# One buffer shared by the activations X and the second state array of the mixer, and distance matrices made inside two mixers

## The chip, the cores and the metric

The kernel runs on one core of one Trainium2 chip. The core has five engines with their own instruction queues: TensorE (PE in the profile; its weight loads are PEld), VectorE (DVE), ScalarE (ACT), GpSimd (POOL) and SyncE (SP). SyncE only issues DMA transfers here, and nearly all of the kernel's transfers go out through it, in the order in which the program lists them. The on-chip memory has 128 partitions (SBUF); matmul results land in PSUM; DRAM lies outside.

The metric is the device time of one execution in microseconds, lower is better. The kernel before takes 8552.56 us, the median of three runs (8548.31 to 8558.02). The profile is one more execution; it took 8578.09 us, with a span of 8576.3 us between its first and last instruction.

## The reference

The input x is 64 samples of 11 x 11 positions with 128 channels, float32. Four layers follow one another, each a mixer and a feed-forward part, both added to x:

```python
for l in range(4):
    x = x + conv_ref[l](_ln_c(x))          # mixer, weights of layer l
    t = x.reshape(64, 121, 128)
    t = t + ffn_ref[l](_ln_t(t))           # l=0: experts, 1 and 2: RNN, 3: spectral
    x = t.reshape(64, 11, 11, 128)
```

The mixer projects each position to 2 x 256 numbers, xc and z. In xc the 121 positions are the channels of the state-space model and the 256 features its length:

```python
xc = silu(conv1d(xc, width 3))                          # (64, 256, 121)
dts, Bs, Cs = split(x_proj(t))                          # for two directions k
delta = softplus(dts @ dt_proj + dt_b)                  # 121 x 256 per sample
h[l] = exp(delta * A) * h[l-1] + delta * Bs * xs        # 16 states per channel
y = sum_n(h * Cs) + Ds * xs;  y = y[0] + flip(y[1])
out = layernorm(y) * gelu(z) @ out_proj_w.T
```

The RNN of layers 1 and 2 multiplies the tokens by W, normalises over all tokens and samples, and runs `yt = sigmoid(wx_t + yt @ V.T)` over the 121 positions one after the other.

The spectral part of layer 3 convolves the tokens with 16 causal filters `phi` in four bands; band i sees the first 121 // (1, 2, 4, 8)[i] positions and has its own matrices `M_phi_plus[i]` and `M_phi_minus[i]` (each 16 x 128 x 128). The bands are added with four weights from a softmax of `log_weights + gumbel`, made hard.

## The kernel before

**Stages.** `metaformer_kernel` (L1340 and after) runs four times: `conv_part`, the mixer, an object `Conv` with a schedule written out by hand; then `FFN[l]`, which is `moe_layer`, `rnn_layer`, `rnn_layer` or `stu_layer`, and whose instructions a scheduler puts in order. Between them the activations lie in DRAM, in seven arrays `mid`. A mixer reads `mid[2l-1]` and writes `mid[2l]`. The feed-forward part opens a buffer `cx.X` of its own (121 partitions x 64 x 128), and its `load()` issues first the weights of the next mixer and then eight loads of 484 KB, from `mid[2l]` to X; at its end eight stores bring X to `mid[2l+1]`.

**The mixer's tiles.** The 64 samples are worked on in NC = 8 chunks of CB = 8. A chunk has two passes, one for each direction, m = 2c + k. A pass goes over the 121 channels in 61 steps of two channels, so that a chunk takes STEPS = 122 steps. The 128 partitions are 16 states x 8 samples. In step g:

- `rows(g + 3)` (L663): TensorE spreads the rows of delta, read from the buffers R, to all states in one of the PSUM tiles `da`; `exps(g + 3)` (L676): ScalarE turns them into the decay. Both run three steps ahead.
- `scan(g)` (L684): VectorE runs the recurrence along the length. Its other input is `ub`, the product of delta and xs spread to all states: `load_u` (L640) fetches a tile of four channels 14 steps ahead into one of seven buffers, by a transfer that repeats the rows, and `times_b` (L652) multiplies it by B on GpSimd 5 steps ahead.
- The states go to `self.H[dq % 2]`, where dq = 0 to 3 counts groups of 16 pairs. There are two such arrays of 128 partitions x 512 x 16; while one fills, `by_c` (TensorE, L705) sums the other over the states into `yb`, `keep_y` (L720 on VectorE, L722 on ScalarE) moves the sums to `yst`, and `store_y` (L737) writes them to DRAM in 16 small transfers, in steps 8 to 11 and 16 to 19 after the end of a second pass.

**The plan.** Everything else of a chunk is laid between these steps by `self.at(step, f)` and `self.lay`; what a step holds is issued after its scan, in the order in which it was laid. `lead(c)` reads the chunk's x (in `begin`, L199), normalises it (`stats` with L208, `scales`, `scales2`, `scales3`) and forms the convolution. `steps(c, k, ...)` makes delta for both directions, as a softplus written in parts, and cuts it into three slices of 16 bits each, `first`, `second`, `third`; with `rest` between them GpSimd subtracts what the slices before already hold. `store` writes the slices to dD and the product u to uD, from where R and `ub` are loaded again. `tail(c - 1)` ends the chunk before: for the first half of its samples the tile `ts` is loaded from sD in step 22 (L439), turned by TensorE in step 31 (L446) and added in the next (L454), and then normalised, gated and projected; the second half follows 22 steps later. All of this shares the five queues with the steps: an instruction that waits holds up whatever stands behind it on its engine.

Before the first step, `run` does `lead(0)` and the first direction of `steps(0, 0, ...)` with nothing beside them. There (`alone`) the tiles relu, abs, w and ln lie in the second array H (`self.spare[1]`), and the bias of the convolution in the first. After the last step, `last(c)` ends the last chunk with all its tiles in the first array H (`self.spare[0]`): `sides`, `load(0)`, `ahead`, `load(1)`, `finish`; `finish` writes the last two pieces to `mid`.

**The feed-forward parts.** All of them normalise X in eight groups of eight samples (`layer_norm`, L52 and L56; two table loads on ScalarE for each group). `rnn_layer` multiplies by W, runs the recurrence (L1186, L1189) and adds the result to X (L1196). `stu_layer` (L1267 to L1329) needs the product K(lag) = sum over k of weight x phi(lag, k) x M[k] for the three short bands: 105 matrices of 128 x 128, the array KD in DRAM. They are made in `stu_matrices`, which the second RNN layer calls. It first forms the weights and a 128 x 105 filter matrix W (22 transfers, some small operations), loads M in eight pieces of 2048 columns, and then hands out 64 pieces of 256 columns, one matmul and one copy on VectorE each; the recurrence takes one piece after every position:

```python
1189                nc.scalar.activation(ys[:, t, :], pst[:, j, :], AF.Sigmoid)
1190                next(beside, None)
```

Eight stores of 840 KB bring the result to KD.

Of the kernel before, what the change touches and what calls it, by code (L numbers as in the profile page):

```python
# [82 lines left out]
class Conv:  # L83
# [75 lines left out]
    def buffers(self, fixed, work, ps_f, dram):  # L159
        nc, NC = self.nc, self.NC  # L160
        self.work = work

        self.H = [fixed.tile([128, 2 * L, 16], F32, name=f"H{i}") for i in range(2)]
        self.spare = [x.rearrange("p a w -> p (a w)") for x in self.H]
        self.da = [ps_f.tile([128, 2, L], F32, name=f"da{i}") for i in range(RING)]
        self.yb = ps_f.tile([128, 8, 2, 2, 16], F32, name="yb")
        nc.vector.memset(self.yb, 0.0)
        self.Cz = [fixed.tile([128, 64, CB], F32, name=f"Cz{i}") for i in range(4)]
        self.t = fixed.tile([128, CB, L], F32, name="t")
        nc.gpsimd.memset(self.t, 1.0)  # L170
        self.xnT = [fixed.tile([C, CB, D + 2], F32, name=f"xnT{i}") for i in range(2)]
        for x in self.xnT:
# [18 lines left out]
    def lead(self, c):  # L191
# [5 lines left out]
        def begin():  # L197
            s["x"] = work.tile([D, CB, C], F32, name="x", bufs=1)
            nc.sync.dma_start(s["x"], self.src(c * CB, CB))  # L199
            if c == 0:  # L200
                s["bias"] = self.spare[0][:D, :L]
                nc.sync.dma_start(s["bias"], self.cx.a[f"L{self.l}_conv_conv_b"].to_broadcast([D, L]))
            s["st"] = work.tile([D, CB, 6], F32, name="st", bufs=1)
            s["r"] = work.tile([D, 2, CB], F32, name="r", bufs=1)

        def stats(b):
            for i in (b, b + 1):
                nc.vector.bn_stats(s["st"][:, i, :], s["x"][:, i, :])  # L208

# [4 lines left out]

        def scales2():
            self.rsqrt(s["r"], s["mv"], self.cx.eps6[:D])

# [3 lines left out]
        def normal(b):  # L221
            x, r = s["x"], s["r"]
            for i in (b, b + 1):
                nc.scalar.activation(
                    x[:, i, :], x[:, i, :], AF.Identity, bias=r[:, 1, i : i + 1], scale=r[:, 0, i : i + 1]
                )
# [47 lines left out]
    def steps(self, c, k, start, apart, late):  # L274
# [4 lines left out]
        for b in range(0, CB, 2):  # L279
# [3 lines left out]
            def tile(n, b=b):  # L283
                if alone:
                    at = 1024 * b + 512 * ("relu", "abs", "w", "ln").index(n)
                    return self.spare[1][:, at : at + 512]
                tag, bufs = ("abs", 1) if n == "ln" else (n, 2 if n == "relu" else 1)
# [310 lines left out]


    def pairs(self):  # L600
        for m in range(2 * self.NC):
# [155 lines left out]
    def run(self):  # L757
# [14 lines left out]
        for c in range(NC):  # L772
            s = STEPS * c
            if c + 1 < NC:
# [64 lines left out]
        ahead()  # L839
        load(1)  # L840
        finish()


# [16 lines left out]
def moe_layer(cx, l, load):  # L860
# [6 lines left out]
    with ExitStack() as ctx:  # L867
# [22 lines left out]
        pooled = keep.tile([C, E, NB], F32, name="pooled")  # L890
        made = load()
        act_tables(nc, 6)

# [150 lines left out]

def stu_matrices(cx, l, keep, work, ps):


    nc, a, ident = cx.nc, cx.a, cx.ident
    p = f"L{l}_ffn_"
    phi, T3, CC, PC = a[p + "phi"], BANDS[3][0], 2048, 256  # L1050
    sw = scale_weights(cx, l, keep)
# [21 lines left out]
    nc.vector.tensor_add(ws[:, 0:1], ws[:, 1:2], mine[:, 3:4])  # L1073
    W = keep.tile([128, R0[3]], F32, name="W")
    for z in range(3):
        nc.vector.tensor_scalar_mul(W[:, R0[z] : R0[z] + NZ[z]], F[:, : NZ[z]], ws[:, z : z + 1])

    def pieces():
        loaded = {}

        def load(c0):
            loaded[c0] = m = work.tile([128, CC], F32, name="m", bufs=3)
            for i in range(4):
                for f0, src in ((0, a[p + "M_phi_plus"]), (16, a[p + "M_phi_minus"])):
                    nc.sync.dma_start(
                        m[32 * i + f0 : 32 * i + f0 + 16], src[i].rearrange("k d e -> k (d e)")[:, c0 : c0 + CC]
                    )

        load(0)
        load(CC)  # L1090
        yield
        for c0 in range(0, C * C, CC):
            if c0 + 2 * CC < C * C:
                load(c0 + 2 * CC)
            ka = work.tile([R0[3], CC], F32, name="ka", bufs=2)
            for j in range(0, CC, PC):
                pa = ps.tile([R0[3], PC], F32, name="pa", tag="mm")
                nc.tensor.matmul(pa, W, loaded[c0][:, j : j + PC], start=True, stop=True)
                nc.vector.tensor_copy(ka[:, j : j + PC], pa)
                yield  # L1100
            nc.sync.dma_start(cx.KD[:, c0 : c0 + CC], ka)

    return pieces()


def rnn_layer(cx, l, load):
# [4 lines left out]
    with ExitStack() as ctx:  # L1111
# [62 lines left out]
        for t0 in range(0, D, TS):  # L1174
# [8 lines left out]
            for j in range(n):  # L1183
# [5 lines left out]
                nc.scalar.activation(ys[:, t, :], pst[:, j, :], AF.Sigmoid)  # L1189
                next(beside, None)  # L1190
        for b in range(0, NB, 4):
# [158 lines left out]
def metaformer_kernel(ctx: ExitStack, tc: tile.TileContext, a: dict, out: bass.AP):  # L1350
# [23 lines left out]

    cx.KD = dram.tile([sum(t1 for _, t1 in BANDS[:3]), C * C], F32, name="KD")
    v, kept, passing, weights = mixer(0)
    weights()()
    passing.close()
    for l in range(4):
        conv_part(cx, v)  # L1380
        kept.close()
        if l < 3:
            v, kept, passing, weights = mixer(l + 1)
        with tc.tile_pool(name=f"X{l}", bufs=1) as pool:
            cx.X = pool.tile([D, NB, C], F32, name="X")
            dst = outr if l == 3 else mid[2 * l + 1]
# [9 lines left out]
            for b0 in range(0, NB, GB):  # L1396
                nc.sync.dma_start(dst[:, b0 : b0 + GB, :], cx.X[:, b0 : b0 + GB, :])
        if l < 3:
# [60 lines left out]
```

## Time and profile before

| | |
|---|---|
| median of 3 runs | 8552.56 us (8548.31 to 8558.02) |
| profiled execution, its own time | 8578.09 us |
| its span | 8576.3 us |
| mean granted TensorE clock | 0.771 |
| busy: TensorE / VectorE / ScalarE / GpSimd | 6028.0 / 6122.9 / 5803.0 / 5868.7 us |
| moved by DMA | 1605.20 MB, mean 187 GB/s |

The stretches of the profiled execution, with busy times of each engine inside them (us):

| stretch | length | PE | DVE | ACT | POOL | DMA share |
|---|---|---|---|---|---|---|
| mixer 0, from 130 on | 1638 | 1136 | 1379 | 1287 | 1395 | 0.89 |
| experts, 1768 to 2050 | 282 | 217 | 104 | 77 | 18 | 0.57 |
| mixer 1, 2050 to 3816 | 1766 | 1188 | 1433 | 1358 | 1462 | 0.85 |
| RNN 1, 3816 to 4028 | 212 | 158 | 60 | 67 | 0 | 0.14 |
| mixer 2, 4028 to 5795 | 1767 | 1198 | 1433 | 1359 | 1463 | 0.87 |
| RNN 2, 5795 to 6088 | 293 | 196 | 92 | 92 | 0 | 0.32 |
| mixer 3, 6088 to 7853 | 1765 | 1200 | 1433 | 1359 | 1463 | 0.85 |
| spectral, 7853 to 8576 | 723 | 677 | 132 | 131 | 0 | 0.10 |

How to read it: a busy share near one in a stretch makes that engine the stretch's limit; where all shares are low, the stretch is set by waits, and the instructions ahead of which an engine stood still have to be found. In the view of the span in 40 slices each digit is the busy share of one slice of 214 us in tenths:

```profile
PE   5667777666666777666567667766577777766999
DVE  5888888843888888872788888883388888886211
ACT  6878888732788788762778888863387888885210
POOL 6888888911888888850888888870388888883000
DMA  6899999945889889960889999972488888896001
```

Lines of the profile that name an operation give line, engine, operation, output tile and input tile. A line of the timeline begins with start and duration in us and ends, in brackets, with the time that the engine stood still before it and what ended that.

### The profile page before, as it was taken

The page shows a single profiled execution, that of the slowest core. Times are in us where ns is not written, and L with a number is a line of the kernel's source. Part 1 is how long each engine was busy: PE and PEld are TensorE (multiplying, and loading weights), DVE is VectorE, ACT ScalarE, POOL GpSimd, SP SyncE. Part 2 cuts the span into 40 slices and gives each one's busy share as a digit, 9 for nine tenths or more (in the row PEclk, how much of TensorE's full clock was granted, in tenths as well). Part 3 has the DMA queues.
Part 4 walks back from the last instruction along what each step waited for, and adds up shares of the span by engine and source line. Part 5 has one row for each costly group of instructions (what it writes and reads, how often), then busy time and mean ns, then how long its engine had stood idle before and what let it go on. Part 6 is the DMA issues. An engine that isn't in the chain of part 4 may idle for free.

```text
span 8576.3 us, 209337 instructions
## 1 busy us (share of the span) xinstructions
PE 6028.0 (70%) x83432; PEld 3462.5 (40%) x83432; DVE 6122.9 (71%) x8654; ACT 5803.0 (68%) x12946; POOL 5868.7 (68%) x3171
## 2 busy tenths in 40 slices
PE   5667777666666777666567667766577777766999
PEld 3333334345333444344233334443334444433445
DVE  5888888843888888872788888883388888886211
ACT  6878888732788788762778888863387888885210
POOL 6888888911888888850888888870388888883000
PEclk7777777777787777776677777766677777777999
DMA  6899999945889889960889999972488888896001
GB/s 171 221 222 226 224 223 222 231 121 167 214 224 224 220 222 223 228 175 23 208 219 225 223 223 223 227 197 62 138 219 219 229 225 224 221 230 151 0 4 36
DMA packets 927599, 1605.20 MB, mean 187 GB/s; under 512 B 140075, under 2 KB 612755, under 8 KB 924755
## 3 DMA queue, kind: packets, MB, share of 16 engines
q1 hardware_dynamic: 925339, 1589.70, 74.3%
q8 instruction: 655, 10.73, 0.6%
q14 instruction: 325, 2.66, 0.1%
q10 hardware_dynamic: 1280, 2.10, 0.1%
HBM read 1301.02 MB, written 290.52 MB: 186 GB/s over the span
## 4 chain that ended last, share of the span: by engine, by line
PE 31%; ACT 20%; DMA 18%; DVE 14%; issue 8%; POOL 7%; SPq 2%; DVEq 0%; POOLq 0%; ACTq 0%
DVE H L684 8%; ACT da L676 7%; DMA ub<-uD 5%; POOL ub L652 5%; PE yb L705 4%; PE da L663 4%; DMA ts<-sD 4%; PE pc L244 3%; DMA uD<-u 3%; PE acc L1290 3%; PE out L1329 2%; PE pu L1287 2%; PE pst L1186 2%; PE po L500 2%; DMA R<-dD 2%
## 5 line engine op out<-in xcount | busy, mean ns | idle before, releaser
L652 POOL TENSOR_TENSOR ub<-ub,Bt 128x1024 f32<-128x1024 f32 (+1 forms) x1984 | 4565.9, 2318 | 749.7 <-DMA ub<-uD 545.4
L684 DVE TENSOR_TENSOR_SCAN H<-da,ub 128x512 f32<-128x512 f32 (+1 forms) x3904 | 4495.2, 1197 | 248.8 <-POOL ub L652 120.6
L676 ACT ACTIVATE da<-da,A 128x255 f32<-128x255 f32 x7744 | 3392.4, 447 | 1122.2 <-PE da L663 936.6
L663 PE MATMUL da<-R,pick 120*128 120x255 bf16 x7744 | 1787.7, 325 | 956.2 <-DVE H L684 761.0
L705 PE MATMUL yb<-H,Cz 128*16 128x64 f32 x65536 | 1722.6, 250 | 557.4 <-ACT yst L722 367.7
L705 PEld LDWEIGHTS yb<-H,Cz 128*16 128x16 f32 x65536 | 1165.4, 111 | 1603.6 <-issue 837.7
L663 PEld LDWEIGHTS <-pick 120*128 120x128 bf16 x7744 | 602.4, 105 | 1657.0 <-issue 781.4
L720 DVE TENSOR_TENSOR yst<-yst,yb 128x512 f32<-128x512 f32 (+2 forms) x640 | 340.5, 549 | 277.4 <-PE yb L705 277.3
L170 POOL MEMSET t<- 128x2048 f32 x4 | 7.2, 1805 | 716.2 <-DMA x<-mid 703.1
L244 PE MATMUL pc<-w_conv,xnT 128*121 128x256 f32 x1344 | 445.5, 429 | 56.4 <-ACT t L248 56.4
L722 ACT COPY yst<-yb 128x512 f32<-128x512 f32 (+2 forms) x640 | 330.8, 543 | 112.0 <-DMA yD<-yst 50.0
L295 PE MATMUL pd<-t,w_dt 122*128 122x512 f32 x480 | 355.4, 832 | 57.4 <-ACT t L255 57.4
L327 POOL TENSOR_TENSOR u<-relu,t 128x512 f32<-128x512 f32 x240 | 307.4, 1281 | 22.2 <-DVE relu L318 22.2
L336 POOL TENSOR_TENSOR d<-relu,d 128x512 bf16<-128x512 f32 x240 | 279.0, 1163 | 59.2 <-ACT d L333 59.2
L1267 DVE COPY U<-pu 128x488 f32<-128x488 f32 x128 | 85.3, 666 | 296.6 <-PE pu L1287 277.2
L1269 ACT COPY U<-pu 128x488 f32<-128x488 f32 x128 | 72.9, 570 | 311.8 <-PE pu L1287 304.9
L330 POOL TENSOR_TENSOR relu<-relu,d 128x512 f32<-128x512 f32 x240 | 279.3, 1164 | 6.6
L244 PEld LDWEIGHTS pc<-w_conv,xnT 128*121 128x121 f32 x1344 | 234.7, 209 | 103.4 <-ACT t L248 82.2
L629 POOL TENSOR_TENSOR Cz<-Cp,own 128x512 f32<-128x512 f32 x256 | 274.3, 1071 | 0.0
L361 PE MATMUL pb<-t,x_bc 121*64 121x512 f32 x256 | 174.6, 771 | 132.0 <-ACT bc L366 100.9
L314 DVE SCALAR_TENSOR_TENSOR pd<-w,pd 128x512 f32<-128x512 f32 x240 | 163.8, 683 | 103.2 <-ACT w L307 103.0
L401 PE MATMUL pg<-xnT,in_zT 128*128 128x484 f32 x256 | 156.2, 695 | 110.1 <-ACT g L412 101.2
(238 smaller groups left out, 7509.7 us busy)
## 6 DMA issues: line engine op xcount, KB each, us to landing
ub<-uD SPq DMA_DIRECT2D x1920, 512.0 KB
dD<-d SPq DMA_DIRECT2D x256, 384.0 KB
R<-dD SPq DMA_DIRECT2D x192, 420.0 KB
uD<-u SPq DMA_DIRECT2D x256, 256.0 KB
sD<-s SPq DMA_DIRECT2D x128, 256.0 KB
yD<-yst SPq DMA_DIRECT2D x512, 60.5 KB
ts<-sD SPq DMA_DIRECT2D x56, 512.0 KB
y<-yD SPq DMA_DIRECT2D x112, 242.0 KB
```

The costliest lines, as they stand in the source:

```text
L244: nc.tensor.matmul(pc, lhs, rhs, start=(j == 0), stop=(j == taps - 1))
L295: nc.tensor.matmul(s["p"], self.w_dt[:, k, :], tb[: D + 1], start=True, stop=True)
L327: nc.gpsimd.tensor_mul(s["u"], s["relu"], tb)
L330: nc.gpsimd.tensor_sub(s["relu"], s["relu"], s["d"][:, 0, :])
L336: nc.gpsimd.tensor_sub(s["d"][:, 2, :], s["relu"], s["d"][:, 1, :])
L652: self.nc.gpsimd.tensor_mul(x, x, self.bc[m, "Bt"].unsqueeze(1).to_broadcast([128, n, L]))
L663: self.nc.tensor.matmul(self.da[g % RING][:, j, 1:], self.pick[:n, d % 5].rearrange("p n b -> p (n b)"), self.R[m, d // 35][:n, d % 35 // ...
L676: self.nc.scalar.activation(x, x, AF.Exp, scale=self.A[:, m % 2, d : d + 1])
L684: self.nc.vector.tensor_tensor_scan(self.H[dq % 2][:, :n, p - DQ[dq][0]], self.da[g % RING].rearrange("p j l -> p (j l)")[:, :n], x.rearra ...
L705: self.nc.tensor.matmul(self.yb[32 * q : 32 * q + 16, slot % 8, :, :, :w], self.Cz[slot // 8][:, place % 64 : place % 64 + 2, :].rearrange ...
L720: nc.vector.tensor_add(dst, dst, src)
L722: nc.scalar.copy(dst, src)
```

## The change

The diff does four things.

**X shares the place of the second H.** A buffer HX of 128 x 8192 numbers is allocated once. The mixer uses it as `H[1]`, the feed-forward part as `cx.X`. X's loads move out of the feed-forward's `load()` into the end of `run`: seven of them behind `load(1)`, the eighth behind `finish()`. `load()` now issues only the next mixer's weights.

**The first chunk comes from X.** In mixers 1 to 3 `begin` of chunk 0 issues no load; statistics and normalisation read `cx.X`. The bias moves to `yst`, the four `alone` tiles to the first array H, since HX now still holds X. An explicit load of ScalarE's table set 6 is added in `scales2` of chunk 0.

**Distance matrices in two mixers.** `stu_matrices` loses its pieces and becomes `stu_filters`, called by `moe_layer` ahead of its normalisations; its W goes to a buffer that lives through the kernel. In mixers 1 and 2 each chunk makes two of the 32 pieces of 512 columns, with 16 loads of 32 KB in step 19, both pieces' matmuls, copies and stores from step 25 on (23 steps later in chunk 0), with tiles that carry the tags relu, w and abs of `steps`. `rnn_layer` has nothing beside its recurrence any more.

**First slices on VectorE.** In the `alone` part, w, `rest` and `third` go from ScalarE and GpSimd to VectorE.

```diff
@@ buffers
-        self.H = [fixed.tile([128, 2 * L, 16], F32, name=f"H{i}") for i in range(2)]
+        self.H = [fixed.tile([128, 2 * L, 16], F32, name="H"), cx.HX.rearrange("p (a w) -> p a w", w=16)]
@@ lead
         def begin():
-            s["x"] = work.tile([D, CB, C], F32, name="x", bufs=1)
-            nc.sync.dma_start(s["x"], self.src(c * CB, CB))
+            s["x"] = s["in"] = work.tile([D, CB, C], F32, name="x", bufs=1)
+            if c == 0 and self.l > 0:
+                s["in"] = self.cx.X[:, :CB, :]
+            else:
+                nc.sync.dma_start(s["x"], self.src(c * CB, CB))
             if c == 0:
-                s["bias"] = self.spare[0][:D, :L]
+                s["bias"] = self.yst.rearrange("p a d -> p (a d)")[:D, :L]
...
-                nc.vector.bn_stats(s["st"][:, i, :], s["x"][:, i, :])
+                nc.vector.bn_stats(s["st"][:, i, :], s["in"][:, i, :])
...
         def scales2():
+            if c == 0:
+                act_tables(nc, 6)
             self.rsqrt(s["r"], s["mv"], self.cx.eps6[:D])
@@ steps
-                    return self.spare[1][:, at : at + 512]
+                    return self.spare[0][:, at : at + 512]
...
-                nc.scalar.activation(s["w"], s["p"], AF.Identity, bias=self.one)
+                if alone:
+                    nc.vector.tensor_scalar_add(s["w"], s["p"], 1.0)
+                else:
+                    nc.scalar.activation(s["w"], s["p"], AF.Identity, bias=self.one)
...
             def rest(s=s):
-                nc.gpsimd.tensor_sub(s["relu"], s["relu"], s["d"][:, 0, :])
+                less = nc.vector if alone else nc.gpsimd
+                less.tensor_sub(s["relu"], s["relu"], s["d"][:, 0, :])
...
             def third(s=s):
-                nc.gpsimd.tensor_sub(s["d"][:, 2, :], s["relu"], s["d"][:, 1, :])
+                less = nc.vector if alone else nc.gpsimd
+                less.tensor_sub(s["d"][:, 2, :], s["relu"], s["d"][:, 1, :])
@@ new function of Conv
+    def matrices(self, i):
+        nc, a, s = self.nc, self.cx.a, {}
+        cols = slice(512 * i, 512 * i + 512)
+        def load():
+            tag = ("relu", "w")[i % 2]
+            s["m"] = self.work.tile([128, 512], F32, name="m", tag=tag, bufs=2 - i % 2)
+            for j in range(4):
+                for f0, M in ((0, a["L3_ffn_M_phi_plus"]), (16, a["L3_ffn_M_phi_minus"])):
+                    nc.sync.dma_start(
+                        s["m"][32 * j + f0 : 32 * j + f0 + 16], M[j].rearrange("k d e -> k (d e)")[:, cols]
+                    )
+        def add():
+            s["p"] = self.ps.tile([R0[3], 512], F32, name="pk", tag="mm")
+            nc.tensor.matmul(s["p"], self.cx.W, s["m"], start=True, stop=True)
+        def leave():
+            s["k"] = self.work.tile([R0[3], 512], F32, name="ka", tag="abs", bufs=1)
+            nc.scalar.copy(s["k"], s["p"])
+        def store():
+            nc.sync.dma_start(self.cx.KD[:, cols], s["k"])
+        return load, add, leave, store
@@ run
+            if self.l in (1, 2):
+                for i in range(2):
+                    for step, f in zip((19, 25, 26, 27), self.matrices(2 * (NC * (self.l - 1) + c) + i)):
+                        self.at(s + step + (3 * i if step > 19 else 0) + (23 if c == 0 else 0), f)
             if c > 0:
...
         load(1)
+        X = self.cx.X
+        for c in range(NC - 1):
+            self.nc.sync.dma_start(X[:, CB * c : CB * c + CB, :], self.dst(CB * c, CB))
         finish()
+        self.nc.sync.dma_start(X[:, CB * NC - CB :, :], self.dst(CB * NC - CB, CB))
@@ moe_layer
         made = load()
+        stu_filters(cx, 3, keep)
         act_tables(nc, 6)
@@ stu_matrices becomes stu_filters(cx, l, keep)
-    W = keep.tile([128, R0[3]], F32, name="W")
+    W = cx.W
...
-    def pieces():
-        loaded = {}
-        def load(c0):
-            loaded[c0] = m = work.tile([128, CC], F32, name="m", bufs=3)
-            for i in range(4):
-                for f0, src in ((0, a[p + "M_phi_plus"]), (16, a[p + "M_phi_minus"])):
-                    nc.sync.dma_start(
-                        m[32 * i + f0 : 32 * i + f0 + 16], src[i].rearrange("k d e -> k (d e)")[:, c0 : c0 + CC]
-                    )
-        load(0)
-        load(CC)
-        yield
-        for c0 in range(0, C * C, CC):
-            if c0 + 2 * CC < C * C:
-                load(c0 + 2 * CC)
-            ka = work.tile([R0[3], CC], F32, name="ka", bufs=2)
-            for j in range(0, CC, PC):
-                pa = ps.tile([R0[3], PC], F32, name="pa", tag="mm")
-                nc.tensor.matmul(pa, W, loaded[c0][:, j : j + PC], start=True, stop=True)
-                nc.vector.tensor_copy(ka[:, j : j + PC], pa)
-                yield
-            nc.sync.dma_start(cx.KD[:, c0 : c0 + CC], ka)
-    return pieces()
@@ rnn_layer
-        beside = stu_matrices(cx, l + 1, keep, work, ps) if l == 2 else iter(())
...
-                next(beside, None)
@@ metaformer_kernel
+    hold = ctx.enter_context(tc.tile_pool(name="hold", bufs=1))
+    cx.HX = hold.tile([128, NB * C], F32, name="HX")
+    cx.X = cx.HX[:D].rearrange("p (b c) -> p b c", c=C)
+    cx.W = const.tile([128, R0[3]], F32, name="W")
...
-            cx.X = pool.tile([D, NB, C], F32, name="X")
...
-            def load():
-                made = weights() if l < 3 else None
-                for b0 in range(0, NB, GB):
-                    nc.sync.dma_start(cx.X[:, b0 : b0 + GB, :], mid[2 * l][:, b0 : b0 + GB, :])
-                return made
-            FFN[l](cx, l, load)
+        FFN[l](cx, l, weights if l < 3 else lambda: None)
```

More of the change, by code (lines that the diff above doesn't have):

```diff
@@ L159, in buffers @@
     def buffers(self, fixed, work, ps_f, dram):
-        nc, NC = self.nc, self.NC
+        cx, nc, NC = self.cx, self.nc, self.NC
         self.work = work
-        self.H = [fixed.tile([128, 2 * L, 16], F32, name=f"H{i}") for i in range(2)]
+        self.H = [fixed.tile([128, 2 * L, 16], F32, name="H"), cx.HX.rearrange("p (a w) -> p a w", w=16)]
         self.spare = [x.rearrange("p a w -> p (a w)") for x in self.H]
@@ L224, in normal @@
                 nc.scalar.activation(
-                    x[:, i, :], x[:, i, :], AF.Identity, bias=r[:, 1, i : i + 1], scale=r[:, 0, i : i + 1]
+                    x[:, i, :], s["in"][:, i, :], AF.Identity, bias=r[:, 1, i : i + 1], scale=r[:, 0, i : i + 1]
                 )
@@ L1042, with stu_filters @@
 R0 = (0, NZ[0], NZ[0] + NZ[1], NZ[0] + NZ[1] + NZ[2])
-def stu_matrices(cx, l, keep, work, ps):
+def stu_filters(cx, l, keep):
     nc, a, ident = cx.nc, cx.a, cx.ident
     p = f"L{l}_ffn_"
-    phi, T3, CC, PC = a[p + "phi"], BANDS[3][0], 2048, 256
+    phi, T3 = a[p + "phi"], BANDS[3][0]
     sw = scale_weights(cx, l, keep)
@@ L1373, in mixer @@
         return v, kept, passing, lambda: v.weights(setup, pool, ps)
-    cx.KD = dram.tile([sum(t1 for _, t1 in BANDS[:3]), C * C], F32, name="KD")
+    hold = ctx.enter_context(tc.tile_pool(name="hold", bufs=1))
+    cx.HX = hold.tile([128, NB * C], F32, name="HX")
+    cx.X = cx.HX[:D].rearrange("p (b c) -> p b c", c=C)
+    cx.W = const.tile([128, R0[3]], F32, name="W")
+    cx.KD = dram.tile([R0[3], C * C], F32, name="KD")
     v, kept, passing, weights = mixer(0)
@@ L1383, in metaformer_kernel @@
             v, kept, passing, weights = mixer(l + 1)
-        with tc.tile_pool(name=f"X{l}", bufs=1) as pool:
-            cx.X = pool.tile([D, NB, C], F32, name="X")
-            dst = outr if l == 3 else mid[2 * l + 1]
-            def load():
-                made = weights() if l < 3 else None
-                for b0 in range(0, NB, GB):
-                    nc.sync.dma_start(cx.X[:, b0 : b0 + GB, :], mid[2 * l][:, b0 : b0 + GB, :])
-                return made
-            FFN[l](cx, l, load)
-            for b0 in range(0, NB, GB):
-                nc.sync.dma_start(dst[:, b0 : b0 + GB, :], cx.X[:, b0 : b0 + GB, :])
+        dst = outr if l == 3 else mid[2 * l + 1]
+        FFN[l](cx, l, weights if l < 3 else lambda: None)
+        for b0 in range(0, NB, GB):
+            nc.sync.dma_start(dst[:, b0 : b0 + GB, :], cx.X[:, b0 : b0 + GB, :])
         if l < 3:
```

## Prediction

> **What bounds the kernel now.** I read the page's slices first, then the boundaries between layers in order of time, then one pass of the mixer loop. The slices show two kinds of time. In the mixers VectorE, ScalarE, GpSimd and the DMA engines are all eight or nine tenths busy; around slices 9, 18, 27 and from 36 on, where the feed-forward layers stand, nearly all but TensorE fall away. There a transfer or a serial chain sets the end.
>
> The two RNN layers run the same code, except that the second also makes the distance matrices. Here is each one's first normalisation, last sigmoid and last addition, as lines of single source lines (first and last start in us):
>
> ```profile
> L52 DVE BATCH_NORM_STATS2 ln_st<-X x64: 259/277/296, 3830.4 to 3862.4; 121x6 f32<-121x128 f32 x64
> L1189 ACT ACTIVATE ys<-pst x121: 224/224/224, 3878.3 to 4012.9; 128x64 f32<-128x64 f32 x121
> L1196 DVE TENSOR_TENSOR X<-X,px x16: 686/687/689, 4014.5 to 4026.9; 121x512 f32<-121x512 f32 x16
> ...
> L52 DVE BATCH_NORM_STATS2 ln_st<-X x64: 258/275/294, 5835.5 to 5884.7; 121x6 f32<-121x128 f32 x64
> L1189 ACT ACTIVATE ys<-pst x121: 224/224/225, 5904.4 to 6043.4; 128x64 f32<-128x64 f32 x121
> L1196 DVE TENSOR_TENSOR X<-X,px x16: 686/687/689, 6074.8 to 6087.2; 121x512 f32<-121x512 f32 x16
> ```
>
> At the boundaries the timeline (start, duration, engine, line) shows what was waited for, in the brackets:
>
> ```profile
> 3816.09 0.24 DVE L157 TENSOR_REDUCE own<-ident 128x8 f32<-128x128 f32 x1
> 3830.42 1.65 DVE L52 BATCH_NORM_STATS2 ln_st<-X 121x6 f32<-121x128 f32 x8 [1.32 <-DMA X<-mid]
> ...
> 5835.52 1.65 DVE L52 BATCH_NORM_STATS2 ln_st<-X 121x6 f32<-121x128 f32 x8 [8.24 <-DMA X<-mid]
> 5838.48 1.28 ACT L56 ACT_TABLE_LOAD   x1
> ...
> 2057.55 1.64 DVE L208 BATCH_NORM_STATS2 st<-x 121x6 f32<-121x128 f32 x8 [7.96 <-DMA x<-mid]
> 4038.06 1.64 DVE L208 BATCH_NORM_STATS2 st<-x 121x6 f32<-121x128 f32 x8 [9.78 <-DMA x<-mid]
> 6097.77 1.65 DVE L208 BATCH_NORM_STATS2 st<-x 121x6 f32<-121x128 f32 x8 [9.13 <-DMA x<-mid]
> ```
>
> Both ways across a boundary the activations are stored and loaded again, and VectorE idles for it. Last, the place in the mixer loop where the new matrix steps land, in its second pass in layer 1:
>
> ```profile
> 2378.72 3.02 SPq L737 DMA_DIRECT2D yD<-yst  x4
> 2382.46 1.56 SPq L613 DMA_DIRECT2D R<-dD  x1
> 2386.46 0.90 SPq L439 DMA_DIRECT2D ts<-sD  x1
> 2396.83 1.07 PE L446 MATMUL pk<-ident,ts 121*128 121x121 f32 x4 [5.52 <-DMA ts<-sD]
> 2397.94 0.66 DVE L454 TENSOR_TENSOR y<-y,pk 128x484 f32<-128x484 f32 x1 [6.70 <-PE pk L446]
> ```
>
> SyncE is issuing almost without a gap and runs behind; ts lands 10.4 us after its issue, and TensorE, then VectorE, stand for it. This place is already late.
>
> **The change, part by part** (times on the profiled execution, 8578.1 us around a span of 8576.3).
>
> *X loaded at the mixer's end.* Seven of X's eight loads (484 KB each) now go out behind the last yD loads, while the mixer finishes; the eighth waits for the last store. VectorE's preparation of the next layer ends at 3816.33 in RNN 1, and the statistics start at 3830.42: 14.1 us go. In the expert layer: 1768.25 to 1783.49, 15.2. In the last layer X was behind 3 MB of M and MU; its first filter matmul is at 7892.1 and needs X and the filters. The filters' last VectorE step ends near 7877.5 and their own DMA does not move forward, so I take 15 (8 to 20). What the loads move past: the last two stores to mid, nothing on the path, and the weights' DMAs, which now wait about 3 us for the eighth load. Their first consumers stand behind two normalised groups.
>
> *Matrices out of RNN 2.* Its start to statistics goes from 5796.34 to 5835.52, 39.2 us, the filters' 22 DMAs and X. Its statistics to last table load before the recurrence (3870.6, 5895.9) take 40.2 us in RNN 1 and 60.3 in RNN 2: 20.1 more, since every normalisation loads two tables, 16 of 1.28. The recurrence up to the last sigmoid is 5.3 longer (142.3, 147.5); from there to the first addition 31.4 against 1.6, leftover pieces: 29.8. The sum is 94.4 us; all of it is alone on the path, so RNN 2 becomes RNN 1.
>
> *The filters in the expert layer.* There ScalarE gets 7 more table loads (by the changed program's instruction order) at 1.28: 9.0 us, and VectorE some 25 operations of 0.16, 4 us. ScalarE is some 55% busy in that phase, so between none and all 13 lands on the path; I take 5. The 22 DMAs stand ahead of the first expert weights on SyncE and cost 16.5 us of issue there (5795.6 to 5812.1 in RNN 2). Cover: the weights issued first have landed by 1830, and the expert matmuls start near 1888; without that cover it would be some 8 us.
>
> The Trainium skill ("ScalarE: Activation LUTs", What ACT_TABLE_LOAD costs) adds a drain of 1.38 us to each switch; the rows here show none, the activation behind the load at 5838.48 starts at 5839.77. With it the seven would be 18.6 instead of 9.0 and that layer would gain nothing.
>
> *First chunk from X.* Three mixers start without the reload: 8.0, 9.8 and 9.1 by the brackets (less 0.0 to 0.2 of other waiting): 26.9 us. The bias load no longer waits and is needed 16 us later. The added table load in scales2 I cost at nothing: in the changed order the same two loads still stand before r's Ln and Exp in these mixers.
>
> *First slices on VectorE.* In the prologue of layer 1 the first dD store is issued at 2099.29, the last at 2114.56. In between GpSimd serialises u (1.28), rest and third (1.15 each) and two waits for dD landings of 2.95. With the subtractions at 0.69 (VectorE's rows of this shape) off GpSimd, the two rounds shorten by about 1.1 and 3.2: 4 us a mixer, 16 in all (bounds 4 and 24). Moving w to VectorE saves ScalarE 0.69 a tile, but ln then waits for another engine: nothing. VectorE gets 12 operations, 8.3 us, in a stretch where it is half idle.
>
> Gains: 14.1 + 15.2 + 15 + 94.4 − 5 + 26.9 + 16 = 176 us (150 to 192).
>
> *The matrices in mixers 1 and 2.* Sixteen times: 16 loads of 32 KB and two stores of 215 KB on SyncE, two matmuls (near 0.8), two copies on ScalarE (0.57). The 16 loads go ahead of R, dD, uD, ub and ts. At RNN 2's spacing of 0.46 us that is 7.4 us of issue, where SyncE has no gap. On the data side 0.94 MB at the rate of RNN 2's burst (193 GB/s at 76% share) is 3.7 us. So ts lands between 2.2 us (its 512 KB share of bytes alone) and 7.4 us (issue alone) later. The second copy reuses the one buffer of the first and waits, three pairs after it, for that store to land: stores here take 6 to 8 us (uD, bcD), 3.5 of which pass meanwhile and three pairs of decay are ready ahead (3.6), so 0 to 4 more; behind it on ScalarE stand the exponentials, and VectorE for them. Lower bound: all of it inside idle time, 0. Upper: 7.4 + 4 + 2.7 of added engine work, 14 us. I take 6 in the fourteen passes with a tail, nearer the DMA row than the issue row since the queue is full there, and 3 in the two first passes, where SyncE waits 18 us on VectorE at that place: 14 × 6 + 2 × 3 = 90 us.
>
> A rule speaks against these loads: the skill's page "DMA: Bandwidth & Descriptors" (Bandwidth) says that transfers below 64 KB are dominated by descriptors, and its table gives about 0.8 us for 32 KB, an estimate between two of its lines. One after the other that is 13 us a pass, 208 in all, and the change would lose some 30 us. No row of this trace has such a load, so it is not settled.
>
> Sum: 176 − 90 = 86 us off. The profiled execution lies 25.5 us above the median of 8552.56; the same sum is taken off both: 8492 profiled, **8467 us** median.
>
> **Rivals.** *The matrix steps hide*: each costs 1.5 us, 24 in all, time 8401. For it: SyncE stands 873 us of 1630 in layer 1's mixer waiting for VectorE, so delays are made up. Against: GpSimd is full outside the stalls. *SyncE's hold starves the loop*: ub and R arrive late as well, GpSimd stops, and each pass pays 13 us: 176 − 208, time 8585, slower. It decides from 11 us a pass (176 / 16). For it: POOL already waits 3.2 us for ub at 2394.55; against: five tiles stand between its load and its use. *The expert layer takes back its gain*: ScalarE's sqrt waits for filter DMAs and the normalisations behind it stand 15 us instead: 25 us worse, 8492. That the change does not do what it says is excluded for RNN 2, whose order has no pieces left.
>
> **How the numbers follow.** Forecast 0.50, hidden 0.22, starved 0.18, expert layer 0.10. The forecast's own range, 3 to 9 us a pass, is 8421 to 8515. The range 8405 to 8560 takes in half of the hidden case and all but the worst of the starved one. A difference of 0.2% (17 us) is about what can be told from none. Faster: 0.50 + 0.22 + 0.10 less 0.06 for bad ends, 0.76; same 0.06; slower 0.18.
>
> **What would show it.** Statistics within 3 us of `own` at RNN layers; RNN 2 from own to last addition as long as RNN 1, near 197 us; no x wait before L208's successor; last dD store 11 us behind the first. In mixers 1 and 2 a pass of 215 us instead of 209, with the wait for ts near 8 us. Wrong if those mixers grow by over 170 us together or by under 40.

## The result and the profile after

The changed kernel takes 8643.77 us, the median of four runs (8635.67 to 8652.78), against 8552.01 before (now four runs): 1.0107 times as long, with an interval of 1.0089 to 1.0124. The forecast was 8467 and faster; it is slower by 92 us. The profiled execution took 8652.78 us around a span of 8651.0.

Stretch by stretch, from the starts of the first normalisation and the first scan and the ends of the last scan and the last addition in the two traces (us; a feed-forward part runs from the mixer's end to the next mixer's first statistics):

| stretch | before | after | difference |
|---|---|---|---|
| experts, RNN 1, RNN 2 | 290.7, 223.1, 303.1 | 296.2, 206.9, 213.2 | +5.5, −16.2, −89.9 |
| spectral part | 723.4 | 704.2 | −19.2 |
| prologues of the four mixers | 67.5, 69.4, 69.5, 71.4 | 66.1, 67.5, 67.2, 68.2 | −8.8 together |
| loops of mixers 0 and 3 | 1647.6, 1645.2 | 1642.2, 1636.2 | −14.4 |
| loops of mixers 1 and 2 | 1649.1, 1648.7 | 1755.2, 1759.2 | +216.6 |

Mixers 0 and 3 do the same work in both kernels; their 14.4 us fit a profiled execution of before that was on the long side of its runs, as its 25.5 us above the median said.

What was to be gained was mostly gained. The groups of single lines in the RNN layers, after (min/median/max ns, first and last start):

```profile
L52 DVE BATCH_NORM_STATS2 ln_st<-HX x64: 255/276/298, 3923.7 to 3949.9; 121x6 f32<-121x128 f32 x64
L1207 ACT ACTIVATE ys<-pst x121: 224/224/225, 3974.8 to 4110.5; 128x64 f32<-128x64 f32 x121
...
L52 DVE BATCH_NORM_STATS2 ln_st<-HX x64: 254/276/296, 6000.3 to 6026.6; 121x6 f32<-121x128 f32 x64
L1207 ACT ACTIVATE ys<-pst x121: 224/224/224, 6053.0 to 6188.8; 128x64 f32<-128x64 f32 x121
L1213 DVE TENSOR_TENSOR HX<-HX,px x16: 686/687/689, 6190.3 to 6202.7; 121x512 f32<-121x512 f32 x16
```

RNN 2 now runs like RNN 1, and its additions follow the last sigmoid at once. The way from the first statistics to the first sigmoid grew, though: 51.1 us in RNN 1 against 47.9 before, and 52.7 in RNN 2. The timeline at the boundaries:

```profile
3920.06 0.24 DVE L157 TENSOR_REDUCE own<-ident 128x8 f32<-128x128 f32 x1
3923.65 1.64 DVE L52 BATCH_NORM_STATS2 ln_st<-HX 121x6 f32<-121x128 f32 x8 [3.35 <-DMA mid<-xo]
...
5991.96 0.24 DVE L157 TENSOR_REDUCE own<-ident 128x8 f32<-128x128 f32 x1
6000.26 1.65 DVE L52 BATCH_NORM_STATS2 ln_st<-HX 121x6 f32<-121x128 f32 x8 [8.06 <-DMA mid<-xo]
...
4125.77 1.58 DVE L211 BATCH_NORM_STATS2 st<-HX 121x6 f32<-121x128 f32 x8
```

The wait for x is gone from the mixers' first statistics (no bracket). The wait for X at the feed-forward's start is not gone: the mixer's last store has taken its place, with 3.4 to 8.1 us. From `own` to the start of the last addition RNN 2 takes 210.7 us, where the prediction's sign was near 197.

The loss lies in mixers 1 and 2, at one place of each chunk. At that place before, GpSimd and SyncE stood as follows:

```profile
2387.96 12.35 SPq L640 DMA_DIRECT2D ub<-uD  x5
2394.55 2.34 POOL L652 TENSOR_TENSOR ub<-ub,Bt 128x1024 f32<-128x1024 f32 x1 [3.22 <-DMA ub<-uD]
```

The five issues in 12.35 us take some 0.5 us each; in between SyncE stands 8.0 us before the last of them. So its queue has hardly a gap up to about 2389, the stretch whose lines the prediction shows, and it has a large one right behind. SyncE's timeline in mixer 1 after, at the same place:

```profile
2383.80 0.89 SPq L775 DMA_DIRECT2D yD<-yst  x2
2384.74 0.74 SPq L620 DMA_DIRECT2D m<-in_L_ffn_M_phi_plus_dram  x1
...
2393.59 0.42 SPq L620 DMA_DIRECT2D m<-n_L_ffn_M_phi_minus_dram  x1
2394.06 0.70 SPq L775 DMA_DIRECT2D yD<-yst  x2
2394.86 0.69 SPq L678 DMA_DIRECT2D ub<-uD  x1
...
2399.18 0.72 SPq L449 DMA_DIRECT2D ts<-sD  x1
...
2403.05 0.35 SPq L633 DMA_DIRECT2D KD<-ka  x1
```

Sixteen loads of m stand for 9.3 us between two stores; the next ub load waits behind them, and the first KD store goes out 6.4 us after its copy on ScalarE had ended (2396.68). GpSimd, ScalarE, TensorE and VectorE in the same timeline:

```profile
2383.56 9.34 POOL L690 TENSOR_TENSOR ub<-ub,Bt 128x1024 f32<-128x1024 f32 x4
2401.89 2.35 POOL L690 TENSOR_TENSOR ub<-ub,Bt 128x1024 f32<-128x1024 f32 x1 [8.99 <-DMA ub<-uD]
...
2396.09 0.59 ACT L630 COPY ka<-pk 105x512 f32<-105x512 f32 x1
...
2415.51 0.59 ACT L630 COPY ka<-pk 105x512 f32<-105x512 f32 x1 [12.14 <-DMA KD<-ka]
...
2417.49 1.21 PE L249 MATMUL pc<-w_conv,xnT 128*121 128x256 f32 x2 [13.01 <-ACT t L253]
...
2419.55 0.66 DVE L464 TENSOR_TENSOR y<-y,pk 128x484 f32<-128x484 f32 x1 [13.93 <-PE pk L456]
```

GpSimd stands 8.99 us for ub (3.22 before). Then ScalarE stands 12.14 us before its second copy, until the store of the first has left the only ka buffer. Behind that copy on ScalarE wait the exponentials and the copy of t (L253); for t TensorE stands 13.01 us, behind it stands the turning of ts (pk), and VectorE, which waits for pk, makes no scan from 2405.6 to 2420.1.

### The profile page after: what moved, and what is told of

Read it like the earlier page. It is cut to its first block, busy times and chain, and to the rows that moved or that the text cites. A ratio compares the mean times of both kernels' runs of the same rounds, so it can differ in the third digit from the quotient of the medians.

```text
span 8651.0 us, 209519 instructions
## 1 busy us (share of the span) xinstructions
PE 6035.8 (70%) x83368; PEld 3463.3 (40%) x83368; DVE 6128.1 (71%) x8638; ACT 5798.6 (67%) x12955; POOL 5834.6 (67%) x3139
## 4 chain that ended last, share of the span: by engine, by line
PE 30%; ACT 19%; DMA 18%; DVE 14%; issue 9%; POOL 7%; SPq 3%; DVEq 0%; POOLq 0%; ACTq 0%
ACT da L714 7%; DVE H L722 5%; DMA ub<-uD 5%; POOL ub L690 4%; PE da L701 4%; PE yb L743 4%; DVE HX L722 4%; PE pc L249 3%; PE acc L1307 2%; PE pu L1304 2%; PE out L1346 2%; DMA KD<-ka 2%; PE pst L1204 2%; DMA ts<-sD 2%; DMA yD<-yst 2%
## 5 line engine op out<-in xcount | busy, mean ns | idle before, releaser
L722 DVE TENSOR_TENSOR_SCAN H<-da,ub 128x512 f32<-128x512 f32 x2048 | 2391.7, 1205 | 110.6 <-POOL ub L690 60.9
L722 DVE TENSOR_TENSOR_SCAN HX<-da,ub 128x512 f32<-128x512 f32 (+1 forms) x1856 | 2117.7, 1187 | 206.9 <-ACT da L714 167.0
L743 PE MATMUL yb<-H,Cz 128*16 128x64 f32 x32768 | 872.2, 255 | 325.9 <-ACT yst L760 248.6
L743 PE MATMUL yb<-HX,Cz 128*16 128x64 f32 x32768 | 852.1, 246 | 195.6 <-ACT yst L760 90.3
L743 PEld LDWEIGHTS yb<-H,Cz 128*16 128x16 f32 x32768 | 607.6, 112 | 927.1 <-issue 536.7
L743 PEld LDWEIGHTS yb<-HX,Cz 128*16 128x16 f32 x32768 | 560.3, 110 | 668.3 <-issue 310.3
L346 POOL TENSOR_TENSOR d<-relu,d 128x512 bf16<-128x512 f32 x240 | 279.1, 1163 | 56.1 <-ACT d L342 55.9
```

What stands on the lines that cost most here:

```text
L346: less.tensor_sub(s["d"][:, 2, :], s["relu"], s["d"][:, 1, :])
L722: self.nc.vector.tensor_tensor_scan(self.H[dq % 2][:, :n, p - DQ[dq][0]], self.da[g % RING].rearrange("p j l -> p (j l)")[:, :n], x.rearra ...
L743: self.nc.tensor.matmul(self.yb[32 * q : 32 * q + 16, slot % 8, :, :, :w], self.Cz[slot // 8][:, place % 64 : place % 64 + 2, :].rearrange ...
```

## The experiments

Two explanations of the 216.6 us. S: the single ka buffer, ScalarE waiting for a store. Q: the queue, 16 loads holding up SyncE. Each ratio is to runs of the kernel before on the same chip, which took 8553 to 8566 us from chip to chip; between chips the ratios compare better than the medians.

**Two places for ka** (`e1`):

```diff
-            s["k"] = self.work.tile([R0[3], 512], F32, name="ka", tag="abs", bufs=1)
+            tag = ("abs", "relu")[i % 2]
+            s["k"] = self.work.tile([R0[3], 512], F32, name="ka", tag=tag, bufs=1 + i % 2)
```

> The second result tile ka of a chunk gets a place of its own (the free one of the two relu tiles), nothing else. In the changed kernel ScalarE stands 166.0 us in 16 waits, 10.4 us a chunk, before its second copy until the first KD store has landed. Theory S (that wait is the price): chunks of mixers 1 and 2 fall from 223 us to 213 to 215, and the time from 8643.8 to about 8500 (8480 to 8530). Theory Q (the 16 loads on SyncE hold up ub, R and ts, as the rival of the prediction had it): the wait goes, but GpSimd's wait for ub stays the limit, chunks stay above 219 and the time above 8585.

8536.18 us, ratio 0.9970 (0.9958 to 0.9983). ScalarE's wait is gone (no bracket at the second copy), but GpSimd still stands for ub at that place:

```profile
2365.67 9.33 POOL L691 TENSOR_TENSOR ub<-ub,Bt 128x1024 f32<-128x1024 f32 x4
2384.19 2.36 POOL L691 TENSOR_TENSOR ub<-ub,Bt 128x1024 f32<-128x1024 f32 x1 [9.18 <-DMA ub<-uD]
2385.83 0.59 ACT L631 COPY ka<-pk 105x512 f32<-105x512 f32 x1
```

**Four loads for sixteen** (`e2`), with the filter matrix's rows put in the same order:

```diff
-            for j in range(4):
-                for f0, M in ((0, a["L3_ffn_M_phi_plus"]), (16, a["L3_ffn_M_phi_minus"])):
-                    nc.sync.dma_start(s["m"][32 * j + f0 : 32 * j + f0 + 16], M[j].rearrange("k d e -> k (d e)")[:, cols])
+            for f0, M in ((0, a["L3_ffn_M_phi_plus"]), (64, a["L3_ffn_M_phi_minus"])):
+                nc.sync.dma_start(s["m"][f0 : f0 + 64], M.rearrange("j k d e -> (j k) (d e)")[:, cols])
```

> The 16 loads of a chunk (32 KB each) become 4 of 128 KB with the same bytes, by another order of the filter matrix's rows; ka keeps its single place. At the 0.46 us spacing of these issues 12 fewer are 5.5 us less SyncE time a chunk. Theory Q: chunks fall by more than 8 us, time below 8515. Theory S: the second copy still waits for the first store, which only goes out some 3 to 5 us sooner, chunks fall by 2 to 5 us, time 8560 to 8610.

8556.58 us, ratio 0.9994 (0.9985 to 1.0004): 87 us gone. ScalarE's wait fell from 166.0 to 106.7 us in all, since the store goes out sooner: in the change it started 3.6 us after its copy (median of 16 chunks), here at once in 14 of the 16. It still held the buffer 12.7 us from its issue to the second copy, against 13.5 in the change.

**Both** (`e3`):

> Both edits at once. If the two costs add, chunks come to within 2 us of the 209.5 of the kernel before and the time to about 8450 (8430 to 8480). If one of them hides behind the other (both theories partly wrong), the time is no better than the better of the two single edits.

8446.77 us, ratio 0.9866 (0.9851 to 0.9881), 1.3% faster than before. The two costs add: 107.6 + 87.2 = 194.8 singly, 197.0 together (by the ratios 117 + 97 against 206). So S and Q were both half right.

**The matrices back in RNN 2** (`e4`; all else as in the change):

> Only the matrices go back to where they were (filters and pieces in RNN 2, 64 pieces beside the recurrence); X shared, first chunk from X and the prologue's VectorE edits stay. By the changed kernel's trace the loops of mixers 1 and 2 are 106.1 and 110.5 us longer than before, RNN 2 with its neighbours 89.9 shorter, the expert layer 5.5 longer. So this kernel should have chunks of 209.5 again and take about 8450 (8430 to 8480), faster than both others. If the time stays above 8530, the loops are slowed by the shared place of H and X and not by the matrices.

8453.22 us, ratio 0.9879 (0.9862 to 0.9895), as expected, with loops of 1639.1 and 1646.3 us. So the shared place costs nothing that shows, and everything but the matrices is worth 106 us. Moving the matrices as e3 does adds hardly more (e3 against e4: 6 us, inside the intervals). By the two traces this is a balance: RNN 2 takes 206 us in e3 against 269 in e4, but the loops of mixers 1 and 2 are 31 us longer and the expert layer 28.

**Each load cut in two** (`e12`, on top of e1):

```diff
+                    for h in (0, 8):
+                        nc.sync.dma_start(s["m"][32 * j + f0 + h : 32 * j + f0 + h + 8], M[j].rearrange("k d e -> k (d e)")[h : h + 8, cols])
```

> The kernel with two ka places and the 16 loads of 32 KB, each load cut in two of 8 rows: 32 loads of 16 KB, the same bytes and the same 2 KB rows. From 16 to 4 loads 89 us went, 0.47 us for each load less in each of 16 chunks. If the number of issues on SyncE is the price, 16 more cost another 16 x 16 x 0.46 = 118 us: about 8655 (8630 to 8680). If it was the size of each transfer or the number of rows in it that mattered only between 32 and 128 KB, or the queue has room, the time stays below 8580.

8608.49 us, ratio 1.0054 (1.0039 to 1.0068): 0.0084 above e1, 72 us. More issues cost more, though less than 118, and the traces show most of why: the loads follow each other at 0.338 us (median) with 8 rows, 0.463 with 16 and 0.694 with 64, so that 32 loads of 8 rows take 3.4 us a chunk more than 16 of 16, some 54 us in all. In the table, the starts of the scans are averaged over chunks 1 to 6 of mixers 1 and 2 (a whole chunk from its first to its last scan's start), and SyncE's time for m, the sum of the loads' own durations, over 16 chunks (us):

| kernel | SyncE's time for m | steps 28 to 34 | whole chunk |
|---|---|---|---|
| before | 0 | 15.8 | 208.9 |
| e3, 4 loads, two ka | 2.7 | 18.6 | 210.1 |
| e1, 16 loads, two ka | 8.0 | 23.8 | 216.3 |
| e12, 32 loads, two ka | 10.5 | 28.3 | 220.8 |
| e2, 4 loads, one ka | 2.7 | 26.0 | 217.9 |
| after, 16 loads, one ka | 7.4 | 31.6 | 224.1 |

The steps outside 28 to 34 take the same time in all six within 2 us, so one place pays for everything. With two ka it pays 2.8, 8.0 and 12.5 us for 4, 16 and 32 loads, about what SyncE needs for them or somewhat more.

**The filters in the expert layer.** e4 has no filters there: 268.7 us; e3 296.3. The seven traces with the filters at this place and X loaded by the mixer (the change, e1, e2, e3, e7, e12, e14) lie between 289.5 and 296.4, 293.4 on average, so e3 is on the long side, and the price is 25 us rather than 28. The intervals of the ratios of e3 and of the next runs overlap; what tells them apart is the length of the layer, from one trace each. On top of e3:

```diff
 e5   stu_filters(cx, 3, keep) called behind the gating loop
 e9   -    nc.scalar.activation(sq, sq, AF.Sqrt)   (twice)
      +    nc.scalar.activation(sq, sq, AF.Ln)
      +    nc.scalar.activation(sq, sq, AF.Exp, scale=0.25)
 e11  e5 + e9, and one load each for F, sq and the sign row sg[64:128]
 e13  e11, and nc.gpsimd.memset(sg[64:128, 1:T3:2], -1.0) in place of the sign row's load
```

> On top of the kernel with two ka places and merged loads, the filters of the spectral part are made behind the gating loop of the expert layer instead of ahead of its normalisations. In the changed kernel that layer took 296.2 us from the mixer's end to the next statistics against 290.7 before, although its own statistics start 8.0 us sooner and the reload behind it (8.0) is gone: some 21 us went to the filters, 13.3 of them in one stand of VectorE for the sign row's transfer, 3.8 of ScalarE for sigma's. If the place of the filters is the cause, the layer comes to about 275 and the time to 8426 (8415 to 8436). If the 22 transfers cost the layer wherever they are issued, or the experts wait for their weights instead, it stays within 8 us of 8447.

8438.22 us, ratio 0.9853 (0.9838 to 0.9868), layer 286.2: at best half of what was hoped for. The scheduler issued the same loads right behind the mixer's weights again, so the late place was late in the program only.

> On top of two ka places and merged loads, sigma to the power 1/4 is formed by Ln and Exp instead of two square roots; the filters stay ahead of the normalisations. The expert layer with filters took 296.3 us against 268.7 in the kernel whose filters stay in RNN 2, 27.6 more, and seven table loads of 1.283 (9.0 us) are among it, since after the square root the normalisations alternate between two tables. If the tables are a third of the price, the layer comes to 286 to 288 and the time to 8438 (8430 to 8443). If only the waits for the transfers count, nothing changes (8447 within 6).

8438.45 us, ratio 0.9855 (0.9840 to 0.9869), layer 285.6: about a third of the price, as expected for the tables.

> The same, with the filters made behind the gating loop as well. That place alone was worth 8.6 us. If the two add, the layer comes to 276 to 278 and the time to 8429 (8420 to 8435); if the late place had gained by the tables alone, it equals the run with Ln and Exp.

8428.79 us, ratio 0.9840 (0.9822 to 0.9857), layer 278.9: the two add, as far as one trace tells.

> The same again, and the filters' 20 loads of phi, sigma and sign rows become 3. The experts' first weights then go out some 17 issues of 0.46 us, 8 us, sooner. If that is what is left, the layer comes to 268 to 271 and the time to 8421 (8412 to 8428), the fastest so far. If it is not, the time is that of the run before within 5.

8438.72 us, ratio 0.9856 (0.9842 to 0.9871): a miss, the layer went up to 293.0. The timeline of this run:

```profile
1776.59 0.66 SPq L1106 DMA_DIRECT2D sg<-in_sgn_dram  x1
1804.53 0.22 DVE L1109 TENSOR_TENSOR F<-F,sg 128x60 f32<-128x60 f32 x1 [22.84 <-DMA sg<-in_sgn_dram]
```

One transfer of 64 x 60 single numbers kept VectorE, and the gating behind it, until 27.9 us after its issue.

> The run with 3 filter loads, with the sign row no longer loaded but written by GpSimd (odd columns to -1). In the run with 3 loads that transfer was issued at 1776.6 and VectorE stood 22.8 us for it until 1804.5, and the expert layer took 293.0 us, 14 more than with 20 loads. If the sign row is what is left of the filters' price, the layer comes to 268 to 272 us, that of the kernel whose filters stay in RNN 2 (268.7), and the time to 8415 (8405 to 8425). If something else holds the layer, it stays above 280 and the time above 8425.

8419.71 us, ratio 0.9845 (0.9830 to 0.9861), layer 266.2: without the sign row's transfer nothing is left of the filters' price. This is the lowest median of all; its ratio does not tell it from those of the other four, but its interval ends at 0.9861, just below e4's, which begins at 0.9862. Whether the rewritten filters would shorten RNN 2 in e4 as well was not tried.

**The other parts, undone one at a time on top of e3.** e6 loads the first chunk from DRAM again, e7 puts w back to ScalarE and rest and third to GpSimd, e8 puts X's loads back behind the next mixer's weights, e14 puts all eight behind the mixer's last store:

```diff
 e14
-        for c in range(NC - 1):
-            self.nc.sync.dma_start(X[:, CB * c : CB * c + CB, :], self.dst(CB * c, CB))
         finish()
-        self.nc.sync.dma_start(X[:, CB * NC - CB :, :], self.dst(CB * NC - CB, CB))
+        for c in range(NC):
+            self.nc.sync.dma_start(X[:, CB * c : CB * c + CB, :], self.dst(CB * c, CB))
```

> On top of two ka places and merged loads, mixers 1 to 3 load their first chunk from DRAM again, as before. The prediction priced that at 8.0 + 9.8 + 9.1 = 26.9 us; if that holds the time is 8474 (8466 to 8481). If the load hid behind the bias load or the table load anyway, it is within 8 us of 8447.

8474.72 us, ratio 0.9891 (0.9874 to 0.9907), 28 above e3 by the medians, 21 by the ratios: near the 26.9 that were predicted.

> On top of two ka places and merged loads, the prologue's w goes back to ScalarE and rest and third to GpSimd. The prediction priced the move at 4 us in each of four mixers, 16 together; the traces before and after show the stretch from first statistics to first scan shorter by 1.4, 2.0, 2.2 and 3.2 us, 8.8 together. By the prediction 8463, by the traces 8456. Within 4 us of 8447 would say that the waits for dD and ub set the prologue either way.

8454.92 us, ratio 0.9875 (0.9860 to 0.9890), 8 above e3 by both, which the overlapping intervals do not tell from 0 or from 16. The four prologues are 11 us longer than in e3's trace, so the traces say 9 to 11, less than the prediction's 16.

> On top of two ka places and merged loads, X is loaded where it was, behind the next mixer's weights at the start of each feed-forward part (H and X still share their place, and the first chunk still comes from X). The prediction's terms are 14.1 for an RNN layer, now twice, 15.2 for the expert layer and 15 for the last: 58 us, so 8505 (8490 to 8520). If the scheduler hides most of the later load behind the layers' own first steps, the time is below 8480.

8465.35 us, ratio 0.9884 (0.9869 to 0.9899). This run did not make X late: the scheduler put its loads among the mixer's last yD stores, where they lengthened the end of each mixer from 38.4 to 45.5 us. That is 28 us in all; the time grew by less, and the expert layer is 17 us shorter in this trace (279.1 against 296.3), for a reason that is open.

> On top of two ka places and merged loads, all eight loads of X are issued behind the mixer's last store instead of seven of them ahead of it. (Where they stood behind the layer's weights in the program, they were put ahead of the mixer's last stores to yD, so that run did not make them late.) By the prediction's terms (14.1, 14.1, 15.2, 15) the time is 8505. By the trace, statistics started 8.4, 7.5, 5.1 and 4.4 us after the mixer's end against 16.7, 15.5 and 25.6 before, since a wait for the last store's landing took the place of the wait for X: 6 to 9 us a layer, 8475 (8465 to 8485).

8448.26 us, ratio 0.9880 (0.9861 to 0.9900). The statistics start 6.7, 6.3, 6.9 and 5.6 us after the mixers' ends, against 8.4, 7.5, 5.1 and 4.4 in e3: 25.5 and 25.4 together. Issuing X before the mixer's end is worth nothing that these runs can tell (1.5 us by the medians, 12 by the ratios, whose intervals overlap); both expectations were too high.

## Why the prediction was wrong, point by point

- **The step that failed**: "I take 6 in the fourteen passes" and 3 in the first two, 90 us in all. The loops grew by 216.6, 13.5 a chunk, near the upper bound of 14 (against e4, whose loops hold no matrices, by 229, 14.3 a chunk). Two terms were mis-sized. The issue of the loads was set "nearer the DMA row than the issue row since the queue is full there"; the issue row was the right one: 12 loads fewer gave 87 us, 5.4 a chunk, 0.45 a load. The store wait was set at "0 to 4 more", from stores that take 6 to 8 us and that start at once. Here the store started 3.6 us late behind the same loads (median; 6.4 in the chunk shown) and held the buffer until 13.5 us after its issue (12.5 in the chunk shown): 10.4 us of standing a chunk, and giving ka a second place took 6.7 us a chunk off the time (e1). The long hold is the larger part, since in e2, where the store starts at once, 6.7 us of standing are left. Why this store takes twice as long as the prediction's stores is open. That "the queue is full there" held up to 2389 only; SyncE's stand of 8.0 us comes after the issue of ts.
- **The filters in the expert layer**, "I take 5", cost 25 to 28 (against e4). The term counted table loads and VectorE's small operations, 13 us at most; it left out that these operations stand ahead of the gating and wait for the sign row.
- **The rivals.** The starved loop was priced at 13 us a pass and 8585, and the expert layer's loss at 25 us: both came, with nearly these sizes, and together. Each had been given a time as if the other stayed away. But only half of the 13.5 is SyncE's hold; the other half is the store wait, which no rival named, so that the starved loop's 13 us is a hit by luck. (The forecast's own range, 8421 to 8515, comes out as 8425 to 8509 where only the 14 passes vary by 3 us, and as 8419 to 8515 where all 16 do; nothing rests on this.)
- **Right, or nearly**: RNN 2 without pieces with its following start (94.4 + 9.1 predicted; 89.9 measured, 96.8 in e3), the first chunk from X (26.9; 28 by the medians), the last layer (15; 19.2). In e4 RNN 2 keeps its pieces and is still 34 us shorter than before, so of the 96.8 some 63 come from the matrices' move and the rest from X and the first chunk.
- **Right in sign, too large**: the prologue, 16 predicted, 9 to 11 by the traces.
- **X loaded at the mixer's end**: an RNN layer was to gain 14.1 because the statistics would follow "within 3 us of own". RNN 1 gained 16.2 in all, 12.0 of which go again in e6, so some 4 are left. The statistics start 10.7 us sooner behind `own` (3.6 against 14.3), but 3.2 us are lost again up to the first sigmoid. What stood behind the old wait, the landing of the last store, was not asked for. By e14 even these come without the early issue; that they come from X no longer standing behind the weights of the layer and of the next mixer fits the order of the issues, but was not tried alone.

The Trainium skill ("DMA: Bandwidth & Descriptors", Bandwidth) says that descriptors dominate transfers below 64 KB; it spoke against the loads, and its sign was right. What these runs show as the price is the loads' issue, 0.34 to 0.69 us each, at a place where SyncE's queue had no gap: with 4, 16 and 32 loads (8446.77, 8536.18 and 8608.49 us) the bytes and the 2 KB rows were the same, and only the number of loads that they were split into differed.

## What to carry to other kernels

Before laying many small transfers into a tuned loop, find where the issuing queue has gaps; where it has none, as here, each transfer can cost its issue time on everything that is queued behind it. Issuing these loads where SyncE stood 8.0 us before was not tried. A result tile with a single place makes the engine that fills it wait for issue backlog plus landing of the store, so count both, and count what is queued on that engine. When two rivals can happen together, price them together.

## What the runs showed that was not expected

- The spacing of loads on SyncE grows with their rows: 0.338 us for 8, 0.463 for 16, 0.694 for 64 rows of 2 KB.
- A transfer of 3840 single numbers held its reader until 27.9 us after its issue; VectorE's work in the expert layer hung on it.
- After the square root, Ln and Exp of the normalisations load tables by turns, while in the expert layer of before none of them loaded one, nor in RNN 1. (Two table loads for each group, said ahead of the prediction of all layers, are right for RNN 2 and for seven of the eight groups of the spectral part.) The timeline of ScalarE in the changed kernel:

```profile
1801.20 1.28 ACT L1109 ACT_TABLE_LOAD   x1 [3.80 <-DMA sq<-in_L_ffn_sigma_dram]
1803.67 1.28 ACT L56 ACT_TABLE_LOAD   x1
...
1824.81 1.28 ACT L56 ACT_TABLE_LOAD   x1
1826.42 1.28 ACT L57 ACT_TABLE_LOAD   x1
```
